# Layers 1 to 3 as one stage in TensorE's source order, with rows taken singly through layer 1 and the layer-2 mixtures

## The chip, the cores and the metric

The kernel runs on one core of a Trainium2 chip. The metric is the device time of one execution in microseconds (us); lower is better. The core has a matrix engine (TensorE, PE in the profile; its weight loads are the row PEld), VectorE (DVE), ScalarE (ACT), GpSimd (POOL) and SyncE (SP), which issues most DMAs. Each engine works through its own queue of instructions in order, and waits on semaphores for the others. Matmul results land in PSUM, which DVE and ACT read.

## The reference

The input is x, 4 rows of 512 tokens of width 128, in fp32. Four layers follow, each as a macaron: half a feed-forward part, attention, half the same feed-forward part, each on a layernorm of x and added to x.

- Layer 0: a mixture of 8 experts (two per token) and a shared expert; attention of 16 heads of width 64. Neither is touched by the change.
- Layer 1: a "LoRA" mixture with one gate per row of x, and an attention *across rows*: for each token position, row s attends to rows 0 to s (16 heads of width 8).
- Layer 2: a mixture with one expert per token (8 experts, hidden width 512, at most 64 tokens per expert and row; later tokens of a full expert are dropped), and causal attention of 16 heads of width 8 over the 512 tokens.
- Layer 3: a channel mix (token shift, squared ReLU, a sigmoid gate), and full attention of 16 heads of width 8.

```python
# layer 2's mixture (token_inputs: rows b, tokens n, width d)
gates = softmax(einsum("bnd,de->bne", token_inputs, Wg)); expert_idx = argmax(gates)
pos = cumsum(mask, axis=1) * mask - mask          # place of a token in its expert, per row
keep = mask * (pos < capacity)                    # capacity = N // E = 64
h = gelu(einsum("becd,edh->bech", expert_inputs, W1))
output = combine(einsum("bech,ehd->becd", h, W2))
# a layer
x = x + 0.5 * ffn(layernorm(x)); x = x + attn(layernorm(x)); x = x + 0.5 * ffn(layernorm(x))
```

So per row the order is: layer 1 (LoRA, attention, LoRA), layer-2 mixture, layer-2 attention, layer-2 mixture, channel mix, layer-3 attention, channel mix. Between rows, only layer 1's attention makes one row wait for another.

## The kernel before

x stays in SBUF as four tiles x[b] of 128 partitions by 4 x 128 (the four token tiles of a row). The program is a sequence of stages with their own tile pools.

**Up to some 742 us** layer 0 runs: router, experts, attention, experts again. In the last experts (`mix2.tiles`, L737 and around) layer 1 of rows 0 to 2 is stepped alongside: units are Python generators, and each `yield` is a place where another unit can put its instructions.

**The stage of layer 1 and the first mixture of rows 0 and 1.** After the experts, with PE's order now that of the source (`manual_schedule` for PE; the other engines' orders are chosen by a scheduler), the live layer-1 rows `l1[b]` are stepped in turns. When row 0 or 1 has finished layer 1 its `route` is stepped too: it finds each token's slot and builds one-hot matrices `disp` (DVE, L1762), with which PE collects the tokens of each expert (L1763) and which are transposed (L1769) to send results back (L1799). The expert matmuls of both rows (L1784, L1792) are in `rest`. Layer 1's attention (`l1_attn`) makes a tile of q, k and v per row (`qkv{s}`, L1231 and L1233), multiplies q with each earlier row's k on POOL (L1253), sums per head on DVE (L1249), and adds the weighted values up on PE (L1276).

**The stage of attention** (`heads_at_once`). Eight attentions k = 0 to 7 follow in a fixed order: layer 2 of rows 0 to 3 (causal), then layer 3 of rows 0 to 3. One attention is 4 groups g of 4 heads. A step is `score` (L1462: four matmuls of 32 rows each into two `big` PSUM tiles, then an Exp on ACT into pT, L1466; causal rows also mask on DVE, L1471) and, two steps later, `value` (L1477: four matmuls into four column strips of one `one` PSUM tile). After a group, ACT copies that tile to U (L1663) and a `turned` unit transposes and normalises it (L1484 to L1488).

Everything else are *streams* beside the attention: `begin{k}` (layernorm, transposes L318, k, q and v: L1436 to L1453), `end{k}` (projection, L1500 to L1506), `mix1` to `mix3` (a layer-2 mixture of a *pair* of rows, `l2_pair`), `channels{b}` (`l3_ffn`, L1943 to L1958). A stream has names that it waits for and a time from which it is thought to be ready. After each score and value, `side(0.8)` takes ready streams in list order until 0.8 us of PE time are filled, by the planner's own clock `now`, which adds the costs that units yield: `yield cost, lag`, PE time and the time until the stream's next step can go. If an attention's `begin` isn't done, `through_with` runs just what it needs, to its end.

A pair mixture: layernorm of both rows, transposes, router logits (L1691), one softmax and argmax for 8 token tiles on DVE, places by two matmuls with triangular ones (L1710, L1711), slots, then eight indirect DMAs from POOL that scatter tokens to DRAM (`pair_x`, L1856), one load X back in expert order (L1864), transposes (L1872), w1 (L1880, 64 recorded matmuls: an fp32 matmul is recorded as two), copies hr (L1882), four GELUs (L1887), w2 (L1896), stores (L1899), eight indirect gathers (L1911) and adds to x (L1906).

The tasks and what they wait for: `mix1` (rows 2 and 3) before `begin2` and `begin3`; `mix2` after `end0` and `end1`; `mix3` after `end2`, `end3` and `mix2`; `channels{b}` after its pair's mixture and its neighbour; `begin4` to `begin7` after their channel mix, and each `begin{k}` after `end{k-2}`. The last attention ends in `end_all`, by halves.

PSUM has three `big` tiles (two banks each) and two `one` tiles (one bank). Layernorm's power of -0.5 is a small POOL instruction (L298) between DVE steps; L294 to L297 are the statistics before it, L307 (DVE) or L305 (ACT) what follows; L329 adds a PSUM tile to x.

## Time and profile before

| | |
|---|---|
| time, median of 3 runs (lowest to highest) | 1439.71 us (1438.87 to 1443.03) |
| the profiled execution: time / span | 1439.91 us / 1438.1 us |
| mean granted TensorE clock | 0.913 |
| busy: PE, PEld, DVE, ACT, POOL | 1205.6, 624.4, 905.3, 664.8, 291.9 us |
| chain that ended last: PE, DVE, issue | 59%, 20%, 8% |
| first and last instruction on L1466 (Exp of layers 2 and 3) | 887.1 and 1409.0 us |
| last L1205 (end of layer 1) | 879.8 us |

The time is that of the whole execution; the span is from the first to the last instruction of the profile. Busy times are of one profiled execution; matmuls are pipelined and their ends are modelled. In the table of windows, each line is a stretch from:to in us with its length, the busy time and instruction count of each engine, the mean granted clock of TensorE (PEclk, 1 is full speed) and the share and rate of the DMA engines. In the chain, each piece has its start, its length and what it was, with "x8" for eight records in a row.

### The profile page before, as it was taken

The numbers are of one execution on the slowest core, as the hardware profiler recorded it, in microseconds if no ns is written. First come the engines' busy times: TensorE is split into PE (matmuls) and PEld (weight loads), VectorE is DVE, ScalarE is ACT, GpSimd is POOL, SyncE is SP. The second block draws the span as 40 slices with busy tenths as digits, with TensorE's granted clock in tenths as the row PEclk, the third lists the DMA queues.
The fourth block names the chain that finished last, engine by engine and source line by source line (L and its number), as shares of the span: only waits on it lengthen the run. The fifth ranks groups of instructions, "written<-read, shape, count | busy, mean of one in ns | idle before, by whom it ended". The sixth has DMA issues, their size and how long they took to land.

```text
span 1438.1 us, 19511 instructions
## 1 busy us (share of the span) xinstructions
PE 1205.6 (84%) x6718; PEld 624.4 (43%) x6718; DVE 905.3 (63%) x2363; ACT 664.8 (46%) x932; POOL 291.9 (20%) x279
## 2 busy tenths in 40 slices
PE   5899899999999999898975498984994699938994
PEld 3456453344253435455553375462444233423332
DVE  4796778989888885966775746554553442234433
ACT  2435446636446362444543234560651256704672
POOL 3420420323104020202334212103022102020100
PEclk9999999999999998989997799996988599968997
DMA  7123121111111110122115000001001000010000
GB/s 276 38 72 105 52 72 59 67 52 59 55 54 59 44 63 16 32 61 61 34 32 173 0 1 1 10 21 29 2 30 30 1 0 31 1 29 1 9 8 17
DMA packets 59949, 63.26 MB, mean 44 GB/s; under 512 B 11073, under 2 KB 51394, under 8 KB 59202
## 3 DMA queue, kind: packets, MB, share of 16 engines
q1 hardware_dynamic: 54210, 50.38, 10.3%
q0 software_dynamic: 5632, 11.55, 2.7%
q8 instruction: 56, 0.92, 0.3%
q14 instruction: 51, 0.41, 0.1%
HBM read 28.48 MB, written 16.65 MB: 31 GB/s over the span
## 4 chain that ended last, share of the span: by engine, by line
PE 59%; DVE 20%; issue 8%; ACT 5%; POOL 4%; DMA 2%; another core or an unknown queue 1%; POOLq 0%; SPq 0%; DVEq 0%; ACTq 0%
PE big L1462 8%; PE big L737 7%; PE one L1477 6%; PE big L1046 6%; PE one L1060 5%; PE one L1089 2%; POOL rs L298 2%; ACT pT L1466 2%; PE one L770 2%; PE big L582 2%; PE big L996 2%; DVE sums L1055 2%; PE one L1896 1%; PE big L1880 1%; DVE st L294 1%
## 5 line engine op out<-in xcount | busy, mean ns | idle before, releaser
L1466 ACT ACTIVATE pT<-big 128x1024 f32<-128x1024 f32 (+1 forms) x224 | 204.7, 969 | 123.8 <-PE big L1462 112.7
L737 PE MATMUL big<-w_w,xsT 128*128 x312 | 152.6, 613 | 0.6 <-issue 0.3
L1047 ACT ACTIVATE pT<-big 128x1024 f32<-128x1024 f32 x128 | 126.1, 1036 | 57.1 <-PE big L1046 53.7
L1462 PE MATMUL big<-qkq,qkk 32*128 32x512 f32 (+3 forms) x1024 | 143.8, 588 | 4.4 <-ACT pT L1466 3.8
L1046 PE MATMUL big<-qk 64*128 64x512 f32 x512 | 128.1, 611 | 5.9 <-DVE U L1082 5.4
L298 POOL TENSOR_TENSOR rs<-rs,root 128x4 f32<-128x4 f32 x51 | 56.9, 1117 | 356.3 <-DVE rs L297 356.0
L1477 PE MATMUL one<-pT,V 128*32 128x512 f32 (+3 forms) x1024 | 120.2, 545 | 3.3 <-ACT xnT L1433 1.6
L818 POOL DMA_INDIRECT yg<-sorted_y,ito x64 | 73.3, 1145 | 221.7 <-DMA sorted_y<-ys 78.3
L1060 PE MATMUL one<-pT,V 128*64 128x512 f32 x512 | 116.9, 598 | 0.0
L562 POOL DMA_INDIRECT sorted_x<-xn,irows x64 | 73.0, 1141 | 70.0 <-DVE share L534 22.4
L1462 PEld LDWEIGHTS big<-qkq,qkk 32*128 32x128 f32 x1024 | 54.2, 194 | 65.5 <-issue 40.4
L1055 DVE TENSOR_TENSOR sums<-sums,pT 128x1024 f32<-128x1024 f32 x64 | 78.1, 1220 | 5.1 <-ACT qk L998 0.5
L1471 DVE TENSOR_TENSOR pT<-pT,w_c_tri 128x256 f32<-128x256 f32 (+1 forms) x96 | 48.6, 512 | 49.8 <-ACT pT L1466 45.1
L1046 PEld LDWEIGHTS big<-qk 64*128 64x128 f32 x512 | 46.6, 187 | 69.5 <-issue 39.9
L737 PEld LDWEIGHTS big<-w_w,xsT 128*128 128x128 f32 x312 | 55.0, 197 | 42.2 <-issue 41.9
L1060 PEld LDWEIGHTS one<-pT,V 128*64 128x64 f32 x512 | 33.9, 136 | 77.1 <-issue 72.1
L582 PE MATMUL big<-xnT,w_w 128*128 128x512 f32 x128 | 61.0, 614 | 6.6 <-DVE u L587 5.6
L744 DVE TENSOR_TENSOR us<-big,t1s 128x1024 f32<-128x1024 f32 (+1 forms) x40 | 47.8, 1194 | 28.1 <-PE one L727 21.5
L1137 ACT COPY U<-one 128x512 f32<-128x512 f32 x32 | 18.8, 587 | 93.0 <-PE one L1060 85.9
L318 PE MATMUL one<-w_c_ident,xns 128*128 128x128 f32 x108 | 22.5, 309 | 39.7 <-DVE xns L307 30.7
L1487 DVE RECIPROCAL inverse<-one 128x16 f32<-128x16 f32 x32 | 8.2, 255 | 73.9 <-PE one L1484 59.8
L1477 PEld LDWEIGHTS one<-pT,V 128*32 128x32 f32 x1024 | 23.3, 111 | 72.2 <-issue 57.8
(353 smaller groups left out, 2238.9 us busy)
## 6 DMA issues: line engine op xcount, KB each, us to landing
other<-qk SPq DMA_DIRECT2D x64, 256.0 KB
xs<-sorted_x SPq DMA_DIRECT2D x78, 64.0 KB
sorted_y<-ys SPq DMA_DIRECT2D x38, 128.0 KB
w_w<-in_w SPq DMA_DIRECT2D x2, 2048.0 KB
w_l_w<-in_l_w SPq DMA_DIRECT2D x2, 2048.0 KB
X<-pair_x SPq DMA_DIRECT2D x3, 512.0 KB
pair_y<-y SPq DMA_DIRECT2D x6, 256.0 KB
w_w<-in_w SPq DMA_DIRECT2D x1, 1152.0 KB
```

The lines of the kernel that those rows point to most:

```text
L298: nc.gpsimd.tensor_tensor(rs, rs, root, ALU.pow)
L562: apart(nc.gpsimd.indirect_dma_start(out=sorted_x[:, :], out_offset=bass.IndirectOffsetOnAxis(ap=irows[:, b, j, t : t + 1], axis=0), in_=x ...
L582: nc.tensor.matmul(pa[:, m, :], lhsT=w["w13"][:, NE, m, odd, c * P : (c + 1) * P], rhs=xTs[b], start=True, stop=True)
L737: nc.tensor.matmul(pa[:, k, :], lhsT=st[u]["xT"][:, k * P : (k + 1) * P], rhs=w["w13"][:, bass.ds(st[u]["e"][k], 1), m].rearrange("p o a b ...
L818: nc.gpsimd.indirect_dma_start(out=y, out_offset=None, in_=sorted_y[: done(b) * P, :], in_offset=bass.IndirectOffsetOnAxis(ap=ito[:, b, j, ...
L1046: nc.tensor.matmul(sT[:, u, :], lhsT=k[r, t * P : (t + 1) * P], rhs=q[r, :], start=True, stop=True)
L1047: nc.scalar.activation(pT[:, :, t % 2, :], sT, AF.Exp, scale=scale)
L1055: nc.vector.tensor_tensor(s, s, pT[:, :, m, :], ALU.add)
L1060: nc.tensor.matmul(po[r, :], lhsT=V[:, t, :], rhs=pT[:, u, t % 2, :], start=(t == 0), stop=(t == NT - 1), tile_position=(0, 64 * u))
L1462: nc.tensor.matmul(sT[j // 2][:, j % 2, c : c + n], lhsT=kT[r, t * P : (t + 1) * P], rhs=qT[r, g, S - n :], start=True, stop=True)
L1466: nc.scalar.activation(p[:, :, :n], s[:, :, :n], AF.Exp, scale=scale)
L1477: nc.tensor.matmul(po[32 * j : 32 * j + 32, S - n :], lhsT=V[k % 2][:, t, NJ * g + j, :], rhs=pT[j // 2][:, j % 2, c : c + n], start=(t == ...
```

## The change

- `l2_pair` becomes `l2_mixed(rows)`, three units `l2_sent`, `l2_taken` and `l2_added`, which can take one row. With one row, w1's matmuls move 64 columns (one expert's tokens) instead of 128, each pair of experts fills one PSUM bank from `spare()` instead of a `big`, and w2 puts two experts into the two 64-column halves of the array. There are four scatters and four gathers per row, one load X and one store. All eight mixtures (layer 2's first and second, of each row) are made so; the one-hot mixture and the pairs are gone from this path. Each row has its own DRAM rooms (`row_x`, `row_y`), half of each zeroed early by 32 more DMAs of 64 KB; the pairs' rooms are still zeroed.
- The stage between layer 0 and attention is gone. What layer 1 has left of each row becomes a stream `first{b}` of `heads_at_once`, followed by `send{n}`, `take{n}`, `mix{n}` and `begin{b}` of that row. `first3` waits for `first0`. When all four are done, `change` releases layer 1's pools and opens a pool `late` for the second mixtures and the channel mixes.
- All PSUM for side steps comes from `spare()`: while attention steps are going it is a `one`; otherwise 2 in 5 are `one` and the rest one bank of a `big`.
- Layer 1: q gets a tile of its own from a shared tag, kept only for its row; the qkv product goes tile by tile; products pr and weighted values pv share five buffers; `held` lets only one row at a time hold values. Some yields are gone, others carry costs.
- Attention: the query of a group is made when the group before it starts (`turn_to`, three buffers of one group) instead of all four in `begin`; pT has 6 buffers instead of 8; U and oT share three.
- The planner: a yield has a third number, the DVE time of the step, which a second clock `free` adds up; a step's result is thought ready a lag after `max(now + cost, free)`. If the next attention isn't made, the planner no longer forces its `begin` through, but takes any stream that is ready, in list order, or the one that is ready soonest. `begin{k}` also waits for `begin{k-1}`.

The diff, cut to its core:

```diff
+    def spare():
+        busy[1] += 1
+        return one() if busy[0] or busy[1] % 5 < 2 else big()[:, 0, :]
+    busy = [True, 0]
...
     def l1_attn(s, w, work, qkv):
-        t3 = work.tile([P, NT, 3 * D], F32, tag=f"qkv{s}", name=f"qkv{s}")
...
+        tq = work.tile([P, NT, D], F32, tag="sT", name="q1", bufs=4)
+        t3 = work.tile([P, NT, 2 * D], F32, tag=f"kv{s}", name=f"kv{s}")
+        for t in range(NT):
+            pq = spare()
+            nc.tensor.matmul(pq[:, : 3 * D], lhsT=xnT[:, t * P : (t + 1) * P], rhs=w["l1_wqkv"], start=True, stop=True)
...
-                yield
+                yield 0.0, 1.3, 0.7
...
+            while held:
+                yield 0.0, 0.5, 0.0
+            held.append(s)
...
     def heads_at_once(rows, w, work, tasks, w3, late):
+        def turn_to(k, g):
+            t = work.tile([P, S], F32, tag="qkq", name="qkq", bufs=3)
+            nc.vector.tensor_scalar(t, queries[k], turn[:, g : g + 1], None, ALU.mult)
+            turns[k, g] = t
...
-            pk = one()
+            pk = spare()
...
-            pT = [work.tile([P, 2, S], F32, tag="pT", name="pT", bufs=8) for _ in range(NJ // 2)]
+            pT = [work.tile([P, 2, S], F32, tag="pT", name="pT", bufs=6) for _ in range(NJ // 2)]
...
         def advance(s):
-            cost, lag = got
+            cost, lag, share = got or (0.0, 1.2, 0.3)
+            start = max(now[0] + cost, free[0])
+            free[0] = max(free[0], now[0]) + share
             now[0] += cost
-            s.ready = now[0] + lag
+            s.ready = start + lag
...
+        while i < len(todo) or waiting or streams:
+            going = i < len(todo) and todo[i][0] in made
+            if going:
+                busy[0] = True
+                k, g, parts, ends = todo[i]
...
+                pTs[i] = score(k, parts)
...
                 side(0.8)
+            if waiting and (len(waiting) > 2 or not going):
+                values()
                 side(0.8)
+            elif not going:
+                busy[0] = False
+                able = [s for s in streams if not s.after]
+                s = next((s for s in able if s.ready <= now[0]), None)
+                if s is None:
+                    s = min(able, key=lambda s: s.ready)
+                    now[0] = s.ready
+                advance(s)
...
+    def l2_taken(w, get, rows, rooms, sent, bufs):
...
         for q in range(NE // 2):
+            h = work.tile([P, 2, NH, nr * CAP], F32, tag=tag("hr"), name="hr", bufs=bufs * NE // 2)
...
+                ph = spare().rearrange("p (j c m) -> p j c m", j=2, c=NH)
             for j in range(2):
                 for c in range(NH):
+                    nc.tensor.matmul(ph[:, j, c, :], lhsT=w["l2_w1"][:, 2 * q + j, c * P : (c + 1) * P], rhs=XT[:, 2 * q + j, :], start=True, stop=True)
             nc.vector.tensor_copy(h, ph)
...
+            for q2 in range(2):
+                py = spare()
+                for q in range(2):
                     for c in range(NH):
+                        for j in range(2):
+                            nc.tensor.matmul(py[64 * j : 64 * j + 64, q * D : (q + 1) * D], lhsT=hs[2 * q2 + q][:, j, c, :], rhs=w["l2_w2"][:, 4 * q2 + 2 * q + j, c, :], start=(c == 0), stop=(c == NH - 1), tile_position=(0, 64 * j))
...
-                routes, early = l2_parts(w2, work, (0, 1))
...
+                def mixture(n, b, after):
+                    first = n < B
+                    send, take, add = l2_mixed(w2, (lambda: work) if first else late, (b,), row_rooms[b], f"slots{n}", 1 if first else 2)
+                    tasks.append((f"send{n}", send, [after] + ([] if first else ["change"]) + ([f"send{n - 1}"] if n else [])))
+                    k = n - 1 if first else n - 2
+                    tasks.append((f"take{n}", take, [f"send{n}"] + ([f"take{k}"] if k >= 0 else [])))
+                    tasks.append((f"mix{n}", add, [f"take{n}"] + ([f"mix{n - 1}"] if n else [])))
+                for b in range(B):
+                    tasks.append((f"first{b}", l1[b] if b in live else iter(()), ["first0"] if b == 3 else []))
+                    mixture(b, b, f"first{b}")
+                    tasks.append((f"begin{b}", None, [f"mix{b}"]))
+                tasks.append(("change", change(), [f"first{b}" for b in range(B)]))
+                for b in range(B):
+                    mixture(B + b, b, f"end{b}")
+                    tasks.append((f"channels{b}", l3_ffn(b, w3, late, False), [f"mix{B + b}", "change"] + ([f"channels{b - 1}"] if b else [])))
+                    tasks.append((f"begin{B + b}", None, [f"channels{b}"]))
```

## The prediction, made before the changed kernel was run

> **What bounds the kernel now.** The page's section 4 puts 59% of the chain of work that ended last on TensorE (PE) and 20% on VectorE (DVE); section 1 has PE busy for 84% of the span. That is an average over stages, so I read the busy time by windows next, cut where the chain changes its lines. The change touches little before about 742 us, where the experts of layer 0 end; these are the windows from there on:
>
> ```profile
> core 0: us, PE busy (x) PEld busy (x) DVE busy (x) ACT busy (x) POOL busy (x), PEclk, DMA share, GB/s
> 742.00:830.00 88.00, 50.78 (x217) 35.23 (x218) 57.11 (x247) 28.61 (x66) 29.30 (x26) 0.73 0.22 75
> 830.00:886.00 56.00, 49.77 (x381) 41.89 (x383) 31.05 (x112) 19.26 (x31) 13.78 (x11) 1.00 0.00 1
> 886.00:953.00 67.00, 60.94 (x542) 29.02 (x546) 38.29 (x112) 41.33 (x55) 10.91 (x10) 0.95 0.06 17
> 953.00:1010.00 57.00, 35.65 (x259) 23.23 (x251) 26.59 (x75) 15.77 (x19) 13.70 (x13) 0.76 0.07 19
> 1010.00:1080.00 70.00, 63.19 (x559) 31.35 (x556) 38.77 (x113) 42.30 (x58) 9.24 (x9) 0.93 0.05 16
> 1080.00:1145.00 65.00, 33.59 (x190) 24.16 (x192) 28.96 (x86) 8.20 (x10) 13.41 (x13) 0.68 0.06 17
> 1145.00:1230.00 85.00, 79.50 (x546) 29.87 (x542) 25.06 (x89) 57.23 (x67) 11.19 (x11) 0.94 0.04 13
> 1230.00:1310.00 80.00, 50.11 (x298) 27.93 (x294) 26.53 (x75) 26.35 (x29) 12.39 (x12) 0.74 0.05 14
> 1310.00:1410.00 100.00, 92.95 (x658) 35.13 (x660) 38.28 (x119) 71.47 (x85) 5.31 (x5) 1.00 0.03 9
> 1410.00:1438.00 28.00, 10.08 (x50) 7.03 (x46) 9.96 (x38) 3.30 (x9) 1.42 (x2) 0.69 0.04 13
> ```
>
> The reader should see three dips, 953, 1080 and 1230, and a slow start at 742: PE busy half the time, at a clock of 0.68 to 0.76. No other engine is full there. PE's work in full-clock microseconds is busy times clock: 37.1 + 49.8 + 57.9 + 27.1 + 58.8 + 22.8 + 74.7 + 37.1 + 93.0 = **458 us**, spread over 668 us.
>
> What a dip is, the chain in order of time shows (start, length, what):
>
> ```profile
> 1081.81 7.16 PE big L1880 x64
> ...
> 1091.35 2.04 PE one L1896 x16
> ...
> 1099.12 2.27 DMA pair_y<-y
> ...
> 1103.54 2.52 DMA yg<-pair_y,islot
> ...
> 1112.39 1.06 POOL rs L298
> ```
>
> It is one pair's layer-2 mixture walked step by step: from end1 (L1506 at 1056.8) to the last gather (1112) it takes 55 us, and from 1080 no attention is left beside it, since both rows that could attend wait for it. The waits view gives the same from PE's side (waiter, releaser: us, times, longest), and one on POOL for later:
>
> ```profile
> PE one L318 <- DVE xns L307: 30.7, 2, 15.3
> PE one L318 <- DVE xn L307: 25.0, 3, 15.4
> POOL yg L1911 <- DMA pair_y<-y: 133.9, 3, 57.7
> ```
>
> So this part is bound by the order of work, not by PE's rate.
>
> **The change part by part.** *Mixtures.* Removed: the one-hot mixture of rows 0 and 1, and three pair mixtures. At full clock a pair costs PE 2 x (0.66 transposes L318 + 0.88 L1691 + 0.43 counts L1710/1711) + 1.3 (L1872) + 7.16 (L1880) + 4 x 2.04 (L1896) = 20.6; three are 61.8. The one-hot costs 16 records of 512 columns at 0.43 (as L737: four in 1.72) = 6.9, L1769 32 x 0.148 = 4.7, L1784 64 x 0.124 = 7.9, L1792 128 x 0.102 = 13.1, L1799 64 x 0.118 = 7.6, and 3.9 for two routers: 44.1. Together 106. Added: eight single-row mixtures. Each still streams all 32 weight tiles of w1, now past 64 columns. Two lines tell what a half-width matmul costs:
>
> ```profile
> 768.66 0.81 PE one L1691 x8
> ...
> 864.12 3.26 PE one L1792 x32
> ```
>
> L1691 moves only 8 columns and takes 0.101 per record; L1880 moves 128 and takes 0.112. So w1 for one row is 64 x 0.101 to 0.112: I take 7.2, as much as for a pair. The w2 step has 64-column weights alternating between two column halves, a form the trace has only with 512 columns (L1060: 16 in 3.58, half of L737's 0.43 each); scaled to 128 it is 0.056, or 3.6 us for 64. Without alternation L1792 takes 0.102, or 6.5 us. I take 4.6, nearer to L1060, which has the same alternation. A row is then 1.97 (transposes, L1691, counts) + 0.63 + 7.2 + 4.6 = 14.4 (13.4 to 16.3), eight are 115: **+9 us of PE** (+1 to +24).
>
> The Trainium skill (TensorE: Matmul & The Clock Gate, LDWEIGHTS) has the weight load grow with columns, P / 1.2 ns: 53 ns for 64, an estimate of 3.4 us for w2. L1792's 102 ns stands against it, L1060's pace for it; by the rule the total would be 11 us lower.
>
> *Other engines.* POOL: 64 instead of 48 indirect DMAs, 16 x 1.03 = 16 us more on 121. DVE: 13 us of small router operations (some 30 x 0.2 per mixture), 7 for hr copies (32 x 0.69 against 12 x 1.225), 3 others: 345 us. ACT: table loads, 12 now (L1887 4, L1466 4, L1785 2, L1262 and L365 1 each; 1.283 a load); at least 16, at most 64 if the four GELUs of a row are split by Exps; I take 24, +15 us, giving 329. All have cover: in the some 600 us I expect they are under 60% busy. Uncovered, the table loads cost up to 15. SP issues 32 more zero fills; today's took about 0.43 each between 84 and 135 us, so 0 to 14, in front of tile loads that nothing on PE waits for now (L737 idles 0.6 us in all). I take 0. Single-row x loads and y stores are smaller, ten more in number, on a queue otherwise empty after 780.
>
> *Moved and waited.* Row b's chain (layer 1, send, take, mix, begin) no longer waits for its neighbours, except that row 3 starts after row 0 and that `held` lets one row at a time hold its values. So attention 0 should start near 825 rather than 887: layer 1 of row 0 ends at 768, the pair's 55 us less half its scatters, gathers and copies is about 42, begin about 15. Row 3's layer 1 ended at 880 among four; later attentions wait for it, but second mixtures do not.
> New waits: every side step now takes its PSUM from `spare()`, which beside attention is the one `one` buffer that the value sum leaves free. The next side step waits until DVE or ACT has emptied it (0.69 plus the queue); behind it on PE stands the next score, and ACT waits for that. Between two side steps lies an attention step of 1.00 to 1.07 that hides most of it. The pT buffers drop from 8 to 6, just the three steps in flight: 0.
> The gathers of a row (L1911) now stand in POOL's queue beside attention, and layernorm powers (L298) and the DVE work after them queue behind.
>
> *The sum.* What rate does PE reach where attention and side steps mix? 886 to 953, 1010 to 1080, 1145 to 1230: (57.9 + 58.8 + 74.7) / 222 = **0.862** full-clock us per us. It holds the `one` waits of today's denser side work, so I take it. Up to 830 I leave the pace as it is (37 done): layer 1's latency rules there. Then (458 + 9 - 37) / 0.862 = 499, to 1329; the last 28 us (end_all) stay: span 1357. The profiled execution took 1439.91 beside a span of 1438.1, and lies 0.2 above the median 1439.71, so 2 more: **1359 us**.
>
> The same page's clock section says that a window of some 3.4 us without work halves the clock and busy ones restore it. Here dips show 0.68 to 0.76, mixed stages 0.93 to 0.95, 1310 to 1410 1.00. If filled stages ran at full clock by the rule, the rate would be the busy share alone, 203.6 / 222 = 0.917, and the total 1329.
>
> **The rivals.** *Denser than thought* (0.13): 1310 to 1410 already mixes channel steps into attention at 0.93. Then 430 / 0.93 = 462: 1322. Against it: that stage holds no mixture.
> *Queues in the way* (0.16): a gather reached early blocks POOL, then a layernorm, then DVE's emptying of PSUM, then PE. In favour: POOL sat 133.9 us at three gathers, at little cost then, as PE had nothing else to do. Price: the store and two gathers of the chain, 2.27 + 2.52 + 2.48 = 7.3, for each of eight mixtures: +58, 1417.
> *Slower* (0.13): PE runs in source order, and eight short mixtures replace four long ones. If a guess of the planner's is wrong, PE stands at the head of a step that isn't ready and attention behind it can't pass. The three dips lost 30 + 42 + 43 us of full-clock work, 38 each. The change loses from (1440 - 1359) / 8 = 10 us per mixture on; at 15, under half of a dip, it gives 1480. Against it: another row's attention is normally in the list.
> *It doesn't do what it says* (0.03): attention 0 starts no earlier, because layer 1 of all rows is put first: near 1440.
>
> **How the numbers follow.** My forecast, 0.55, lies at 1315 to 1400 by itself: rate 0.82 to 0.92, w2 from 3.6 to 6.5, loads and zero fills uncovered or not. The range from 1295 to 1435 takes in the first two rivals and leaves out the last two. About 0.3% (4 us) is what a measurement can tell from no change. Faster: 0.55 + 0.13 + 0.16 = 0.84; same: 0.02; slower: 0.14.
>
> **What would show it.** Right: the first L1462 near 825; no stretch of 50 us with PE below 60% between there and the end; total full-clock PE work some 9 us above before; w1 at 0.10 to 0.11 per record. Wrong: waits of PE on DVE or ACT for a PSUM buffer that total over 60 us; POOL at gathers with L298 late behind them; table loads over 30; a PE wait of over 10 us that recurs at every mixture.

## The result and the profile after

The changed kernel is no faster: 1441.3 us against 1439.86 (medians of 16 executions each), ratio 1.0012 with a 95% interval of 0.9989 to 1.0035. The forecast was 1359. The profiled execution took 1436.15, with a span of 1434.4.

The windows of the kernel after, cut as before (columns: start and end in us, length, busy us and instructions of each engine, granted clock of TensorE, DMA share, GB/s):

```profile
core 0: us, PE busy (x) PEld busy (x) DVE busy (x) ACT busy (x) POOL busy (x), PEclk, DMA share, GB/s
742.00:830.00 88.00, 58.36 (x329) 43.47 (x330) 61.77 (x240) 29.07 (x61) 38.06 (x34) 0.75 0.26 84
830.00:886.00 56.00, 42.63 (x237) 26.38 (x237) 37.92 (x137) 26.73 (x38) 19.44 (x18) 0.78 0.05 15
886.00:953.00 67.00, 56.80 (x494) 42.12 (x494) 29.87 (x98) 25.63 (x38) 11.86 (x11) 0.80 0.06 17
953.00:1010.00 57.00, 47.99 (x386) 24.03 (x378) 36.90 (x146) 26.75 (x37) 13.81 (x13) 0.88 0.05 14
1010.00:1080.00 70.00, 55.47 (x428) 43.29 (x427) 30.64 (x103) 30.22 (x40) 11.52 (x12) 0.78 0.07 20
1080.00:1145.00 65.00, 56.16 (x506) 37.04 (x505) 37.24 (x128) 31.22 (x41) 14.52 (x14) 0.90 0.08 25
1145.00:1230.00 85.00, 75.19 (x511) 39.34 (x507) 35.00 (x121) 50.14 (x56) 18.06 (x18) 0.88 0.07 19
1230.00:1310.00 80.00, 70.37 (x513) 30.03 (x516) 26.76 (x81) 53.24 (x62) 8.18 (x8) 0.97 0.03 7
1310.00:1410.00 100.00, 89.95 (x624) 33.51 (x617) 35.84 (x114) 64.68 (x78) 5.30 (x5) 0.96 0.03 9
```

In windows cut as before the three dips are gone: none is below 66% busy. But the stretches that were full are no longer full: 886 to 953 held 60.94 us at a clock of 0.95 and holds 56.80 at 0.80. Busy times clock gives 435.6 full-clock us from 830 to 1410, where the forecast put 430. So the work is nearly as forecast, and the pace is not: 435.6 / 580 = **0.751** instead of 0.862. At 0.862 the same work would have taken 505 us. That is 75 of the 77 us by which the profiled span misses the forecast 1357. A window's mean clock makes this product rough; added up between the changes of the granted clock, the work in these 580 us is 430.8. TensorE was busy for 494.6 of them, so it stood idle for 85 us and lost some 64 to the half clock.

Cutting the same trace where the scores of one row's attention begin and end (line L1483 of the changed kernel) shows where the pace goes:

```profile
906.00:945.00 39.00, 30.95 (x188) 25.78 (x188) 15.79 (x55) 8.77 (x15) 11.86 (x11) 0.69 0.09 28
945.00:977.00 32.00, 30.25 (x314) 15.47 (x309) 19.08 (x73) 22.27 (x29) 5.61 (x5) 0.95 0.06 18
977.00:998.00 21.00, 14.26 (x80) 8.98 (x76) 13.05 (x54) 3.87 (x8) 3.28 (x3) 0.76 0.00 1
998.00:1029.00 31.00, 27.42 (x260) 13.67 (x260) 17.49 (x51) 21.05 (x27) 5.19 (x5) 1.00 0.06 18
1029.00:1084.00 55.00, 42.98 (x280) 36.87 (x280) 24.67 (x93) 15.97 (x22) 11.26 (x11) 0.69 0.07 20
1084.00:1116.00 32.00, 29.25 (x310) 15.16 (x304) 18.33 (x55) 20.88 (x27) 8.44 (x8) 1.00 0.12 35
1116.00:1159.00 43.00, 34.85 (x254) 28.22 (x253) 23.00 (x88) 13.42 (x19) 12.45 (x12) 0.80 0.08 24
1186.00:1403.00 217.00, 192.86 (x1388) 78.87 (x1384) 77.69 (x242) 140.13 (x163) 24.14 (x23) 0.96 0.04 12
```

Every second line holds scores and reaches 0.85 to 0.91; the four lines between hold none and reach 0.52 to 0.65 (30.95 x 0.69 / 39 and so on). All stretches with scores (857 to 906 and 1159 to 1186 among them) are 388 us at 0.845; those without, with 830 to 857, are 185 us at 0.56. Between the first score and the last, the kernel before has three stretches without, 164 us at 0.35; the kernel after has four, 158 us at 0.56. So the dips have become shallower, not shorter in sum, and windows cut as before hide them.

### The profile page after: what moved, and what is told of

The parts are those of the page before. It is cut to its first block, busy times and chain, and to the rows that moved or that the text cites. A ratio compares the mean times of both kernels' runs of the same rounds, so it can differ in the third digit from the quotient of the medians.

```text
span 1434.4 us, 20432 instructions
## 1 busy us (share of the span) xinstructions
PE 1232.9 (86%) x7062; PEld 659.9 (46%) x7062; DVE 918.5 (64%) x2476; ACT 684.7 (48%) x949; POOL 307.3 (21%) x295
## 4 chain that ended last, share of the span: by engine, by line
PE 59%; DVE 21%; issue 9%; ACT 5%; POOL 3%; DMA 1%; another core or an unknown queue 0%; POOLq 0%; DVEq 0%; SPq 0%; ACTq 0%
PE big L1483 7%; PE big L745 6%; PE one L1498 6%; PE big L1054 6%; PE one L1068 5%; PE one L1925 3%; PE one L1097 2%; POOL rs L306 2%; ACT pT L1487 2%; PE one L778 2%; PE big L1004 2%; DVE sums L1063 2%; PE big L1925 1%; PE one L326 1%; DVE st L302 1%
## 5 line engine op out<-in xcount | busy, mean ns | idle before, releaser
L1055 ACT ACTIVATE pT<-big 128x1024 f32<-128x1024 f32 x128 | 125.9, 1034 | 57.6 <-PE big L1054 53.4
L1483 PE MATMUL big<-qkq,qkk 32*128 32x512 f32 (+3 forms) x1024 | 139.6, 573 | 11.6 <-ACT pT L1487 5.7
L306 POOL TENSOR_TENSOR rs<-rs,root 128x4 f32<-128x4 f32 x51 | 57.6, 1131 | 423.0 <-DVE rs L305 410.2
L1498 PE MATMUL one<-pT,V 128*32 128x512 f32 (+3 forms) x1024 | 123.5, 557 | 3.8 <-ACT xnT L1997 1.8
L570 POOL DMA_INDIRECT sorted_x<-xn,irows x64 | 71.7, 1120 | 70.3 <-DVE share L542 22.7
L1483 PEld LDWEIGHTS big<-qkq,qkk 32*128 32x128 f32 x1024 | 52.3, 190 | 69.0 <-issue 35.2
L1925 PE MATMUL one<-XT,w_l_w 128*128 128x64 f32 x384 | 58.3, 318 | 7.7 <-DVE hr L1926 2.8
L1925 PEld LDWEIGHTS one<-XT,w_l_w 128*128 128x128 f32 x384 | 55.4, 230 | 17.7 <-DVE hr L1926 5.7
L1886 POOL DMA_INDIRECT row_x<-xns,islot x32 | 32.3, 1011 | 116.1 <-DVE islot L1882 106.8
```

Of the source, the lines that this page charges most:

```text
L306: nc.gpsimd.tensor_tensor(rs, rs, root, ALU.pow)
L570: apart(nc.gpsimd.indirect_dma_start(out=sorted_x[:, :], out_offset=bass.IndirectOffsetOnAxis(ap=irows[:, b, j, t : t + 1], axis=0), in_=x ...
L1055: nc.scalar.activation(pT[:, :, t % 2, :], sT, AF.Exp, scale=scale)
L1483: nc.tensor.matmul(sT[j // 2][:, j % 2, c : c + n], lhsT=kT[r, t * P : (t + 1) * P], rhs=turns[k, g][r, S - n :], start=True, stop=True)
L1498: nc.tensor.matmul(po[32 * j : 32 * j + 32, S - n :], lhsT=V[k % 2][:, t, NJ * g + j, :], rhs=pT[j // 2][:, j % 2, c : c + n], start=(t == ...
L1925: nc.tensor.matmul(ph[:, j, c, :], lhsT=w["l2_w1"][:, 2 * q + j, c * P : (c + 1) * P], rhs=XT[:, 2 * q + j, :], start=True, stop=True)
```

## The experiments

Each ratio is to the kernel before, run beside it on the same chip (its median there: 1447 to 1450, for the last three experiments 1421). Differences between experiments are differences of ratios, times 1440; that a ratio is the same on another chip is assumed. Attentions are numbered in their order, 0 to 3 the causal ones of rows 0 to 3, 4 to 7 those of layer 3; line numbers are the changed kernel's.

**1. w1 at 128 columns.** In the gaps the w1 matmuls stand out: 32 of them in 7.03 us at 928, in 7.09 and 7.03 at 1059, twice the 3.6 that the forecast gives for 32.

```
-  nc.tensor.matmul(ph[:, j, c, :], lhsT=..., rhs=XT[:, 2 * q + j, :], ...)
+  k = j * NH + c                  # the last of the eight moves 64 columns
+  nc.tensor.matmul(ph.rearrange("p j c m -> p (j c) m")[:, k : k + 2, :], lhsT=...,
+                   rhs=XT[:, 2 * q + j : 2 * q + j + 1, :].to_broadcast([P, 2, CAP]), ...)
```

> The changed kernel with the 64 tokens of a row presented twice to w1, so that each of its 64 matmuls moves 128 columns instead of 64; the next matmul writes over the second copy, and the values are the same. Clock theory (half-width matmuls behind full 128x128 weights leave TensorE at its half clock): 32 records that took 7.0 in the stretches at half clock take 3.6 to 3.9 everywhere, all w1 of the eight rows some 58 us instead of 79, the granted clock between 740 and 1230 rises, and the time falls by 15 to 25 us, to 1415 to 1425. Rival (the half clock comes from the waits around, not from the matmuls' shape): the 7.0 us groups stay where they are, and the time stays at 1441 plus or minus 5.

Measured: 1425.6 us, ratio 0.985 (0.9794 to 0.9906): 23 us less than the changed kernel. All w1 took 68.9 us instead of 80.0. In the two listings of one line's instructions (duration in ns: least, median, most), the changed kernel first and this one second, the same 32 matmuls of row 2 are seen, and 15 of the 32 behind them:

```profile
L1925 PE MATMUL one<-XT,w_l_w x32: 275/275/422, 923.4 to 927.9; 128*128 128x64 f32 x32
L1925 PE MATMUL big<-XT,w_l_w x32: 421/421/421, 928.1 to 934.7; 128*128 128x64 f32 x32
```

```profile
L1929 PE MATMUL one<-XT,w_l_w x32: 222/275/377, 930.7 to 934.2; 128*128 128x128 f32 x28, 128*128 128x64 f32 x4
L1929 PE MATMUL big<-XT,w_l_w x15: 222/275/328, 934.3 to 935.9; 128*128 128x128 f32 x14, 128*128 128x64 f32 x1
```

With 64 columns the clock falls in the middle of the row; with 128 it holds. The mean granted clock of the four executions was 0.923 to 0.927, against 0.899 to 0.917 in the 16 of the changed kernel. So a higher clock goes with the shorter time. But w1 itself gives only 11 of the 23 us, and w1 did not fall to the 58 that were expected. That the 64 columns caused the fall isn't shown either: in experiments 11 and 14 the same 64 matmuls of row 2, with 64 columns, took 7.4 us at full clock (the last section has the line).

**2. The kernel before with w1 at 64 columns.**

```
-  rhs=XT[:, 2 * q + j, :]         # 128 columns: two rows
+  rhs=XT[:, 2 * q + j, :CAP]      # 64 columns; the copy out of PSUM takes them twice
```

> The kernel before with w1 of its three pair mixtures moving only the first row's 64 of 128 columns; the copy out of PSUM takes them for both rows, so the second row's hidden values are the first's, and nothing else differs. Clock theory: the groups of 64 records that took 7.2 in the dips take up to 14 (0.22 a record), since nothing lifts the clock, and the time rises by 10 to 20 us, to 1450 to 1460. Rival (a record of w1 costs its weight load, whatever moves behind it, and the clock comes back in any case): 6.5 to 7.2 as before, and the time stays within 4 us of 1440.

Measured: 1453.89, ratio 1.0052 (1.0021 to 1.0083), 7 us. But w1 has no part in them: the line took 22.4 us in all, 22.7 before, and 64 records stood at 7.26 even at 1091. Half-width alone does not halve the clock: here it follows a stretch at full clock. What raised the time by 7 us I did not find.

**3. Begin steps that don't wait for the mixture.**

```
-  tasks.append((f"begin{b}", None, [f"mix{b}"]))
+  tasks.append((f"begin{b}", None, [f"send{b}"]))
-  (f"channels{b}", ..., [f"mix{B + b}", "change"] + ...)
+  (f"channels{b}", ..., [f"send{B + b}", "change"] + ...)
```

> The changed kernel in which each row's begin step and each row's channel mix wait only until the row's tokens are sent to the experts, not until the mixture's result is added; every instruction is still issued, but attention and channel mix of a row take x without that mixture. Starvation theory (one row's chain of mixture and begin is longer than the attention there is beside it, so TensorE runs out of attention): the chain is some 35 us shorter eight times, the gaps without attention at 905 to 943, 1041 to 1083 and 1137 to 1158 close, and the time falls to between 1350 and 1390. Rival (TensorE's own rate where everything mixes, its clock and its waits for PSUM, bounds the stage): the gaps go but the work spreads, and the time stays above 1420.

Measured: 1470.49, ratio 1.0174 (1.0106 to 1.0243), slower by 23 us than the changed kernel. Attention 0 started at 834 and attention 1 at 914, but attentions 2 and 3 at 997 and 1083, as in the changed kernel, and row 3's layer 1 ended later still (its last router matmul at 1013 instead of 952). The gaps moved and did not close.

**4. The planner without VectorE's running total.**

```
-  start = max(now[0] + cost, free[0])
+  start = now[0] + cost
```

> The changed kernel whose planner no longer counts VectorE's share when it says when a stream's next step is due (start is now plus cost, without the running total for VectorE); only the order of TensorE's steps differs. Theory of held-back streams (that total runs 3 to 6 us ahead and delays the chains, which are what starves attention): chains end earlier, and the time falls by 10 to 30 us, to 1410 to 1430. Rival (the total is a fair picture of VectorE): TensorE stands more often at a step whose input is not there, waits on VectorE grow, and the time rises by 5 to 30 us, to 1446 to 1470.

Measured: 1469.1, ratio 1.0145 (1.0088 to 1.0202). That is 19 us worse than the changed kernel: the total is of use as it is, and the theory of held-back streams is out.

**5. Layer 1 of all rows first.**

```
+  # inside manual_schedule for PE
+  while live:
+      for b in list(live):
+          if (b < 3 or 0 not in live) and next(l1[b], live) is live:
+              live.remove(b)
   for b in range(B):
       tasks.append((f"first{b}", l1[b] if b in live else iter(()), ...))
```

> The changed kernel with the four rows' layer 1 finished together, one step of each row in turn, before the stage with mixtures and attention starts; mixtures, attention and channel mixes stay as the change has them. Theory of the late row (as a stream beside attention, row 3's layer 1 ends at 975 instead of 880, and everything behind it comes later): row 3's layer 1 ends before 900, attention 3 starts 30 to 60 us sooner than at 1084, and the time falls by 10 to 40 us, to 1400 to 1430. Rival (what counts is when the first attention can start, and layer 1's latencies are well hidden beside it): attention 0 starts 30 us later than at 857, everything else follows it, and the time rises by 10 to 30 us, to 1450 to 1470.

Measured: 1472.14, ratio 1.0189 (1.0109 to 1.0268). Row 3's last layer-1 router stood at 860 instead of 952, yet the first attention only started at 943. In this order of work, layer 1 beside attention is worth 25 us; this part of the change does what it says.

**6. Row 0's second mixture freed from row 3's first.**

```
-  [after] + ... + ([f"send{n - 1}"] if n else [])
+  [after] + ... + ([f"send{n - 1}"] if n % B else [])
-  [f"take{n}"] + ([f"mix{n - 1}"] if n else [])
+  [f"take{n}"] + ([f"mix{n - 1}"] if n % B else [])
```

> The changed kernel in which row 0's second mixture no longer waits in the task list for row 3's first one (neither for its sending nor for its adding); nothing else is edited. Theory of the chained mixtures (after the change row 0's second router stands at 1038, 118 us after row 0's attention ended, since it follows row 3's router at 989 and its scatters): row 0's second router comes at 985 to 1000, the first attention of layer 3 starts 25 to 40 us sooner than at 1159, and the time falls by 10 to 35 us, to 1406 to 1431. Rival (TensorE is busy with other rows' work in that time anyway): the router comes sooner, but the time stays within 5 us of 1441.

Measured: 1413.72, ratio 0.9753 (0.9702 to 0.9804): **37 us** less than the changed kernel, from two entries in a list of names. The router (line L1713) of row 0's second mixture, in the changed kernel and then in this one:

```profile
L1713 PE MATMUL one<-w_l_wg,xnT x8: 256/256/277, 1038.1 to 1038.9; 128*128 128x8 f32 x8
```

```profile
L1713 PE MATMUL one<-w_l_wg,xnT x8: 256/256/277, 1009.4 to 1010.2; 128*128 128x8 f32 x8
```

It comes 29 us sooner, though not by 1000, and attention 4 at 1153, only 6 sooner. Most of the gain lies behind that: row 1's second begin step (k = 5) stood at 1200 instead of 1221, and the last scores ended at 1384 instead of 1403, on a chip that took 7 us longer for the kernel before. So the edit's 37 us are measured, but the way to them is not the expected one. The windows of the changed kernel, then of this one:

```profile
830.00:1150.00 320.00, 262.36 (x2077) 175.58 (x2077) 176.35 (x626) 141.14 (x193) 72.15 (x68) 0.83 0.06 18
1150.00:1350.00 200.00, 177.48 (x1205) 79.05 (x1205) 74.76 (x243) 126.03 (x143) 29.54 (x28) 0.91 0.04 12
```

```profile
830.00:1150.00 320.00, 263.19 (x2112) 172.29 (x2113) 178.94 (x631) 146.68 (x199) 76.31 (x72) 0.84 0.07 20
1150.00:1350.00 200.00, 183.86 (x1349) 81.27 (x1348) 80.07 (x258) 142.19 (x162) 26.97 (x26) 0.97 0.04 11
```

Busy times clock over length: 0.680 and 0.808 become 0.691 and **0.892**. From 1150 to 1350 the stage now beats the forecast's 0.862; from 830 to 1150 hardly anything has changed.

**7 and 8. Together with the other edits.**

```
experiment 7: the edits of 6 and 1
experiment 8: the edits of 6, 1 and 5
```

> The edit that frees row 0's second mixture from row 3's first, together with the one that presents a row's 64 tokens twice to w1. If the two causes (held-back mixtures, half clock) are separate, their gains add: the time is that of the first edit less 12 to 18 us. If the half clock was only a mark of the starved stretches, the second adds under 6 us to the first.

Measured: 1410.25, ratio 0.9745 (0.9692 to 0.9799), no different from 0.9753. The 23 us of experiment 1 do not add to those of 6: with row 0 freed, w1 took 68.5 us at 64 columns already. The two gains overlap, so neither is the share of one cause.

> All three edits: layer 1 of the four rows finished together first, row 0's second mixture freed from row 3's first, w1 moving 128 columns. Theory (late row, chained mixtures and half clock are three causes of their own): the lowest time of all, 1360 to 1400, with no stretch without attention over 30 us after the first attention starts. Rival (layer 1 in front costs more than it gives): higher than the kernel with the last two edits alone by 10 to 30 us.

Measured: 1437.77, ratio 0.9934 (0.9908 to 0.9959): 27 us worse than experiment 7, as in 5.

What is left is the stretch from 830 to 1150. The other experiments go after it.

**9. Early begin steps on top of 6** (the edits of 3 and 6).

> The kernel that frees row 0's second mixture from row 3's first (1413.7), and in it begin steps and channel mixes that wait only until the row's tokens are sent, not until the mixture is added; all instructions are issued, but attention and channel mix take x without that mixture. Starvation theory, in the form that is left (a row's mixture and begin last longer than one row's attention, and the earlier trial of this edit failed only because row 3's mixture held up the second ones): attention starts sooner for every row, and the time falls by 15 to 50 us, to 1365 to 1400. Rival (what is late is not the mixtures but layer 1 of rows 2 and 3, which loses its slots to attention): attentions 2 and 3 start no sooner than before, and the time stays above 1405 or rises.

Measured: 1463.68, ratio 1.0101 (1.0053 to 1.015), 50 us worse than 6. Attention 0 starts at 833, row 2's router goes from 901 to 965 and row 3's last layer-1 router from 959 to 1020. Attention that comes sooner takes TensorE from the rows behind.

**10. Layer 1 listed ahead of the mixtures**, on top of 6.

```
   for b in range(B):
       tasks.append((f"first{b}", ..., ["first0"] if b == 3 else []))
+  for b in range(B):
       mixture(b, b, f"first{b}")
```

> The same kernel (1413.7) with all four rows' layer 1 listed ahead of the mixtures, so that where several steps are due the planner takes layer 1's; nothing else is edited. Theory of the late row (row 3's layer 1 ends at 975 for want of slots): it ends before 940, attention 3 starts 20 to 40 us sooner than at 1086, and the time falls by 5 to 25 us. Rival (its latencies set its end, slots are free): row 3's layer 1 ends at 965 to 980 as before, and the time stays within 5 us, or rises where row 0's mixture is now second.

Measured: 1435.5, ratio 0.9897 (0.9842 to 0.9952). Row 3's last layer-1 router came at 921 instead of 959, so slots, not latencies, had held it. But attention 0 fell back from 863 to 904, attention 3 came at 1100 instead of 1086, and the time rose by 21 us.

**11. The second mixtures as two pairs**, on top of 6.

```
+  for i in range(2):
+      send, take, add = l2_mixed(w2, late, (2 * i, 2 * i + 1), pair_rooms[i], f"slots{B + i}", 1)
...
-  [f"mix{B + b}", "change"]
+  [f"mix{B + b // 2}", "change"]
```

> The same kernel (1413.7) with the four second mixtures as two pairs (rows 0 and 1, rows 2 and 3), as the kernel before has them; the first four stay single. If the added work of single rows counts most (w1 streamed twice, some 7 us a row): 4 to 6 times 6 us less PE work, and the time falls by 5 to 15 us. If independence of the rows counts most: attention 4 waits for attention 1's end and a pair's chain, a stretch of 30 us or more without attention appears behind attention 3, and the time rises by 10 to 35 us, to 1424 to 1449.

Measured: 1424.27, ratio 0.9817 (0.9773 to 0.9861), 9 us worse than 6, with intervals that overlap. Busy time times clock from 742 to the end was 532.28 x 0.87 = 463 us instead of 548.04 x 0.87 = 477, and a gap of 46 us stood behind attention 3. Less work and a longer gap are both seen; which of them weighs more these runs don't tell.

**12. The second mixtures in the first ones' buffers**, so that they need not wait for row 3's layer 1, on top of 6.

```
-  l2_mixed(w2, (lambda: work) if first else late, ..., 1 if first else 2)
+  l2_mixed(w2, (lambda: work), ..., 1)
-  [after] + ([] if first else ["change"]) + ...
+  [after] + ...       # and a mixture waits while another holds the buffers
```

> The same kernel (1413.7) with the second mixtures in the first ones' buffers, so that they need not wait until all four rows have left layer 1 and its memory is given back; they take turns with the first ones. Theory of the chained mixtures, one link further (row 0's attention ends at 924, its second router comes at 1004, since it waits for row 3's layer 1): row 0's second router comes at 940 to 960, attention 4 starts 15 to 40 us sooner than at 1153, and the time falls by 5 to 25 us, to 1389 to 1409. Rival (row 0's second mixture then takes slots, buffers and POOL from row 3's first, which is later for it): the time stays within 5 us of 1414 or rises.

Measured: 1445.07, ratio 0.9973 (0.9947 to 0.9999), 32 us worse. Row 0's second router did come at 943, as expected, but attention 3 started at 1131 instead of 1086: row 0's second mixture went ahead of row 3's first.

**13 and 14. Are mixtures held up by their buffers?** Two sets for all mixtures, on top of 8; then one after the other for the second ones, on top of 6.

```
13: -  k = n - 1 if first else n - 2
    +  k = n - 2                        # all in the memory that layer 1 leaves
14: +  k = n - 1 if n != B else -1
```

> Set against the kernel with all three edits (layer 1 first, second mixture freed, w1 at 128 columns: 1437.8): once layer 1 is done its memory is free, so here all mixtures, the first four too, have two sets of buffers, and a row's experts wait for the row before the last, not for the last. Theory of the serial mixtures (one set makes the begin steps follow at 51 to 66 us: 924, 975, 1038, 1102): they follow at 30 to 45, the gaps without attention shrink under 10 us, and the time falls by 20 to 60 us, to 1378 to 1418. Rival (TensorE's slots beside attention, not the buffers, set the pace of a mixture): the begin steps stay 50 or more apart, and the time stays within 10 us of 1438.

Measured: 1441.52, ratio 0.9964 (0.9935 to 0.9992). The begin steps stood at 928, 980, 1040 and 1097. In this order the buffers set nothing.

> Set against the kernel that only frees row 0's second mixture (1413.7): the second mixtures, too, take their experts one row after the other, although they have two sets of buffers. Theory of the serial mixtures: their begin steps, 1147, 1199, 1263, 1320, are spread further, a gap without attention appears behind 1150, and the time rises by 10 to 40 us. Rival (PE is full there anyway, at 0.89, and rows leave attention 55 us apart): within 5 us of 1414.

Measured: 1411.24, ratio 0.9743 (0.9696 to 0.9789), equal to 6.

**15. Twice the room for side steps**, on top of 7.

```
-  side(0.8)
+  side(1.6)
```

> Set against the kernel with the second mixture freed and w1 at 128 columns (1410.3): between two attention steps the planner may place side steps worth 1.6 us of TensorE instead of 0.8. Theory of the slots (chains lose time because each of their steps waits for a slot between attention steps): attention stretches, the gaps between 917 and 1144 shrink to under half, and the time falls by 10 to 30 us. Rival (chains wait for their own inputs, slots are free; in the trace attention runs alone between 878 and 898): the order hardly changes, and the time stays within 8 us of 1410.

Measured: 1425.48, ratio 0.985 (0.9806 to 0.9893), 15 us worse than 7. The order did change: the first three gaps went from 28, 23 and 46 us to 31, 27 and 32, and attention 3 started at 1094 instead of 1081.

**16 to 18. VectorE's mask, and the length of attention**, all on top of 7. From 830 to 1150 the costliest group on VectorE is the triangle mask of the causal attentions (busy us, mean ns, then the idle time of VectorE ahead of it and what ended it; experiment 7):

```profile
L1492 DVE TENSOR_TENSOR pT<-pT,w_c_tri 128x256 f32<-128x256 f32 (+1 forms) x96 | 48.3, 511 | 44.4 <-ACT pT L1487 41.0 <-issue 3.0
```

```
16: -  if rows[k][2]:                   # the mask
    +  if False:
17: +  to_mask.append((p, parts))       # issued behind the next score
18: -  rows = [(n, b, causal) for n, causal in (("l2", True), ("l3", False)) for b in range(B)]
    +  rows = [(n, b, False) for n in ("l2", "l3") for b in range(B)]
```

> Set against the kernel with the second mixture freed and w1 at 128 columns (1410.3): the triangle mask of the causal attentions is left out (keys of the same 128 tokens that come later are not hidden), nothing else. Theory of VectorE's queue (its mask operations, 48 us, and the 41 us for which they stand waiting for Exp, delay the small operations that release TensorE): the rate from 860 to 1144 rises from 0.73 to 0.80 or more and the time falls by 20 to 50 us, to 1360 to 1390. Rival (VectorE's lateness costs nothing, chains are bound elsewhere): it falls by less than 8 us.

Measured: 1381.45, ratio 0.9715 (0.9672 to 0.9757). The time lies in the expected range, but on this chip the kernel before took only 1421 too: against 0.9745 the ratio is 0.3% lower, inside the intervals. Against experiment 17, which has all of the mask's operations and ran beside it, 7 us: 48 us of VectorE's work are worth little.

> Set against the same kernel (1410.3): each score's triangle mask is issued one score later, when its Exp is long done, so that VectorE no longer stands waiting for it; the same operations in all. Theory of VectorE's queue, waiting part: the 41 us of waiting at the mask fall under 10, and the time falls by 10 to 30 us. Rival (only the order changes, or the mask now comes too late for the value product, which waits for it): within 6 us, or slower.

Measured: 1388.75, ratio 0.9759 (0.9719 to 0.98): no gain. VectorE still stood 38 us at the mask, so the edit did not take the wait away, and tells nothing of its price.

> Set against the same kernel (1410.3) and the one without the mask: the first four attentions, too, take all keys for all queries, as the last four do (no mask, 16 full steps a row instead of 12 partial ones). That adds 4 x 12.8 = 51 us of full-clock work to TensorE: a row's 4 x 1280 columns at 2.14 per 512 become 4 x 2048. Starvation theory (attention is too short for a row's chain, and what is added falls into the gaps): beside the kernel without the mask the time rises by less than 20 us, and the rate from 860 to the last first-layer attention exceeds 0.82. Rival (TensorE and what feeds it are the limit): the time rises by 45 to 65 us beside the kernel without the mask.

Measured: 1431.69, ratio 1.0066 (1.004 to 1.0093): 50 us more than experiment 16, for 51 us of added work. The gaps between attentions 0 and 4 did shrink, from 114 us in all to 54, but the scores of attentions 0 to 3 now span 244 us in all instead of 144, twice the added work. The windows of this kernel reach 275.55 x 0.93 / 320 = 0.80 and 0.86; those of experiment 16 reach 0.78 and 0.90:

```profile
830.00:1150.00 320.00, 275.55 (x2021) 142.69 (x2019) 128.44 (x509) 194.32 (x231) 74.82 (x71) 0.93 0.06 19
1150.00:1350.00 200.00, 177.40 (x1307) 78.09 (x1306) 74.24 (x255) 134.00 (x152) 26.22 (x25) 0.97 0.03 10
```

So a gap is not free room. If it were, most of the 51 us would have vanished in it; instead the side steps that had filled the gaps moved in between the scores and lengthened them.

## Why the prediction was wrong, step by step

**Second mixtures do wait for row 3.** The prediction said of row 3's layer 1: "later attentions wait for it, but second mixtures do not." The diff says otherwise in two places. `send{n}` waits for `send{n - 1}`, so row 0's second (n = 4) for row 3's first, and `change` waits for all four rows' layer 1. I read the chain as one of rows 0 to 3 and did not carry it across n = 4. In the trace row 0's attention ended at 920 and its second router came at 1038. Experiment 6 cuts the first of the two waits (and that of `mix4` for `mix3`) and gets 37 us back, 45% of the miss of 82. How much of that is the wait itself and how much the new order behind 1150 is not separated. Cutting the other as well (experiment 12) costs more than it gives.

**The rate was read from the wrong windows.** 0.862 came from three windows of before in which a row's attention stands in the list throughout. That holds after, too: 0.845 wherever scores run. I applied it to all of 830 to 1410, on the argument that "another row's attention is normally in the list". It was not for 185 us, at 0.56; at 0.862 their 103.5 us of work take 120, so 65 us are lost there. With experiment 6 the rate from 1150 on is 0.892, and the forecast's pace is shown to be within reach there. From 830 to 1150 it stayed at 0.69 to 0.72 in experiments 6, 7 and 14. On the chip of experiments 16 to 18 it was 0.75 to 0.80, with 0.75 in experiment 17, which gained nothing; experiment 7 was not run there, so how much of this is the chip's is not known.

**What holds that stretch is open.** The best versions stand at 0.9743 to 0.9753 where 1359 would be 0.944: some 44 us. No gain came from any of these: begin steps freed from mixtures (3, 9), layer 1's priority (5, 8, 10), buffers (13, 14), room beside attention (15), and little from leaving out VectorE's mask (16). Each edit that brought one row forward sent another back: attention 0 by 30 us for row 3's layer 1 by 61 (9), row 3's layer 1 by 38 for attention 0 by 41 (10), row 0's second router by 66 for attention 3 by 45 (12). Added attention cost its full length (18). That fits a stretch limited by what TensorE's single written order gets through, waits and low clock included, and not by any one chain; but this is argued, not shown, since every edit also reshuffled the whole order.

**The row's chain was undersized.** Layer 1 of row 0 ended near 768, as said. From row 0's router to the first begin matmul it took 777 to 850, 73 us, where 42 and part of 15 were put; attention 0 started at 857 instead of 825. Row 3's layer 1 ran to about 970 instead of 880, since beside attention its steps wait for slots (10 shows it).

**The work.** PE +9 was forecast, within +1 to +24; by the windows from 742 to 1410 it is 479 against 458, +21. Added up between the changes of the granted clock, the same traces give 476 against 466, +9: the size of the work was right, and the product of busy time and mean clock is the rougher of the two. The step "w1 for one row takes as much as for a pair" holds only at full clock (32 in 3.74 to 3.79); at the clocks that were granted w1 took 80.0 us in all against 57.6, or 0.156 a record where 0.10 to 0.11 was named as a mark. w2 came in cheaper than put: 32 in 1.97, so 3.9 a row instead of 4.6. The Trainium skill's rule for weight loads (TensorE: Matmul & The Clock Gate, LDWEIGHTS), 53 ns for 64 columns, came nearer to these 0.06 us a record than my 0.072.

**The marks that were named.** No 50 us below 60%: held, and it was too weak a mark, since a low clock at 80% busy costs as much. First score near 825: missed. Waits for a PSUM buffer over 60 us: no. From 742 to 1410 TensorE stood at most some 42 us for a copy out of PSUM whose result the waiting step doesn't read; the largest part, 12.7 us in four waits, was that of layernorm's transposes (L326) for the attention's normalising (L1509), and ahead of w1 2.8 us were for the copy of hr. A wait of over 10 us at every mixture: no, the longest of all was 6.4. Table loads over 30: yes, 32 in the stage, 16 for GELU and 12 for the attention's Exp. Eight of them stand in the chain that ended last, with 8 us in all, so they are a small part of the miss. Gathers with layernorm powers late behind them: POOL stood 52.5 us at gathers, and the powers then found their input late, not their queue.

**The rivals.** "Slower" named the mechanism that came nearest: fixed order, with steps reached before they are ready. Its price, 10 us per mixture and the change is lost, is what happened in sum, but not by single waits, so the agreement of the price is luck. TensorE's idle time from 830 to 1150 even fell, from 71.9 to 57.6 us; the clock there fell with it, 0.87 to 0.83.

## What to carry to other kernels

Read a task list's names across the point where a second round begins: two entries with `n - 1` that tie the first task of round two to the last of round one cost 37 us here. When a rate is taken from windows of the old trace, say what was present in them, and forecast apart the time in which it will be absent. Before calling a gap free room, put work into it: here 51 us of it cost 50.

## What the runs showed of the hardware

TensorE's clock fell to half in a stretch in which TensorE was nearly always busy. First, two windows of the changed kernel inside row 2's w1, 64 columns behind each 128x128 weight tile. Then all of the same 64 matmuls in experiment 14, with 64 columns too, and the second of the first windows in experiment 1, with 128 columns (there w1 starts at 930.7):

```profile
923.00:928.00 5.00, 4.59 (x32) 4.60 (x32) 2.95 (x14) 0.63 (x1) 1.05 (x1) 0.78 0.02 3
928.00:935.00 7.00, 7.00 (x34) 6.96 (x33) 2.38 (x9) 1.26 (x2) 0.00 (x0) 0.50 0.00 0
```

```profile
929.00:937.00 8.00, 7.36 (x64) 7.22 (x64) 5.53 (x24) 1.89 (x3) 1.05 (x1) 1.00 0.01 2
```

```profile
928.00:935.00 7.00, 5.89 (x50) 5.65 (x51) 6.14 (x26) 2.51 (x5) 1.05 (x1) 1.00 0.01 2
```

In the changed kernel the granted clock goes from 0.78 to 0.50 while TensorE is busy for 4.59 of 5 and then for 7.00 of 7 us. Just ahead of w1 it stood for 0.95 us, but so it did in experiments 1 and 14 (0.94), where the clock stayed up. The Trainium skill (TensorE: Matmul & The Clock Gate, Part 1) gives the half clock to an idle window of some 3.4 us; here it fell without one: in the 20 us ahead TensorE's longest standstill was 2.4 us. The width doesn't decide it: with 64 columns the clock fell in the changed kernel and in experiment 6 (32 in 7.03 us), and stayed in experiments 11, 14 and 2 (64 such matmuls in a row in 7.26 us at a granted clock of 1.00). What decides it stays open.

Weights of 64 columns on alternating halves of the array ran at 0.06 us a matmul of 128 columns (32 in 1.97, experiment 6 at 953, at full clock), half the 0.12 of w1's full tiles (32 in 3.74).
